# A three-layer graph network on one core: the rows of 57 gathered tiles are fetched one by one by SP and ScalarE

## The chip, the cores and the metric

The kernel runs on one core of one Trainium2 chip. The metric is the device time of one execution in microseconds (us), the median of several runs. The profile is one further execution, recorded by the hardware profiler.

Names of the profile: PE is TensorE (PEld its weight load), DVE is VectorE, ACT is ScalarE, POOL is GpSimd, SP is SyncE. A name with a q behind it (SPq, ACTq, DVEq) is that engine's instruction queue: DMA issues, register work, semaphore waits.

## The reference: what is computed

`x` has 6250 rows (nodes) of 256 floats; 100,000 edges, sorted by their target node, have a source, a target, one of 3 types and 32 attributes. All is float32.

```python
def _gcn_forward(x, edge_index, edge_type, edge_attr, weights, roots, biases, edge_w, edge_b):
    src, dst = edge_index
    ew = edge_attr @ edge_w + edge_b
    rel_masks = [(edge_type == i).astype(x.dtype) for i in range(3)]
    inv_cnt = [1.0 / jnp.maximum(segment_sum(m, dst, n), 1.0) for m in rel_masks]
    for l in range(3):
        residual = x
        msg = relu(x[src] * ew)
        out = zeros((n, 256))
        for i in range(3):
            h = segment_sum(msg * rel_masks[i][:, None], dst, n) * inv_cnt[i][:, None]
            out = out + h @ weights[l, i]
        x = residual + relu(out + x @ roots[l] + biases[l])
    return x
# the result is layernorm(x + _gcn_forward(x, ...))
```

The part that matters here is `x[src]`: in each of the three layers, 100,000 rows of 1 KB are fetched by index.

## The kernel before, in words

The edges are cut into 782 tiles of 128 edges (one edge per partition), two tiles to a pair, 391 pairs; two pairs lie together in one buffer `xs` of 128 x 2 x 2 x 256 floats (L895, eight such buffers). The function `layer` is called three times. Its main loop (L760) is written out in full and runs over steps `it`; each step reduces one pair, in the order `order`: pairs 64 to 390, then 63 down to 0. All instructions are recorded in this program order and each engine runs its own in that order; nothing reorders them later. So an engine that waits in one instruction holds back all that stands behind it on that engine.

What one step holds, with the pair that it serves counted from the step:

- `gather`, nine pairs ahead (L763, L898): GpSimd issues two indirect DMAs, each of which fetches 128 rows of `x` (first layer) or of `x_mid` (the layer before, written to DRAM) by the indices in `src_io`. The first six pairs of a layer are gathered at the end of the layer before.
- `load_at` on SP, when the pair nine ahead opens a new group of eight pairs (L559): the edge attributes, 256 KB. In the first layer ScalarE's queue loads blocks of `x` now and then (L545).
- `reduce`, this pair (L640): TensorE multiplies the messages `xs` with one-hot matrices `oh` of 120 columns (3 types x a window of 40 nodes) into PSUM `h_p`, two buffers.
- `make_ew`, four pairs ahead, once for four pairs (L594): TensorE makes the edge weights `ew_p` of four pairs in four PSUM banks from `at`.
- `add`, the pair before (L649): VectorE adds `h_p` to its window of `acc`, at a place held in a register; the registers are loaded eight at a time (L652).
- `weigh`, three pairs ahead, once for two pairs (L623): VectorE multiplies `xs` by `ew_p`, one instruction of 128 x 512 for each pair (L626); ScalarE takes the Relu of both pairs (L628).
- for one of 49 blocks of 128 nodes, about every eighth step: `root_turn` (TensorE transposes `x_all`, L664), one step later `root_turned` (ScalarE copies the result to `t_s`, L668), one step later `root_mul` (TensorE, L672), one step later `root_keep` (VectorE, L675).
- for a block whose edges are done: `node_mul` (TensorE, L687) and `node_end` (VectorE, L718 and L721), each in two parts; SP writes the block to `x_mid` (L723), or in the last layer to the output (L740) after the norm; ScalarE clears its place in `acc` (L704, L707). In the last layer SP also loads the block of `x` again (L747).
- `one_hot`, two pairs ahead, once for two pairs (L630): VectorE makes `oh`, in the first layer ScalarE a bfloat16 copy `oh_b` (L638).

Of the kernel before, what the change touches and what calls it, by code (L numbers as in the profile page):

```python
# [8 lines left out]
F32 = mybir.dt.float32  # L9
BF = mybir.dt.bfloat16  # L10
I32 = mybir.dt.int32
# [431 lines left out]
def ordered_path(ctx, tc, x, attr_laid, A, weights, roots, biases, edge_w, edge_b, out, src, src_i, seg, place_i, consts, x_root,  # L443
# [6 lines left out]
    nc = tc.nc  # L450
    P = 128
    N, D = x.shape
# [10 lines left out]
    order, _, moved, least, most = schedule(N, E, 1)  # L463
# [19 lines left out]
    with tc.tile_pool(name="bias_s", bufs=1) as bias_s:  # L483
# [9 lines left out]
        rows_of = bias_s.tile([P, D], F32, name="rows_of")  # L493
# [34 lines left out]
    edge = ctx.enter_context(tc.tile_pool(name="edge", bufs=2))  # L528
# [7 lines left out]
    def first_of(p, n):  # L536
        return p == 0 or order[p - 1] // n != order[p] // n
# [19 lines left out]
    def load_at(g):  # L557
        at = edge.tile([P, GROUP // OCT, 2, P], F32, name="at", bufs=3)
        nc.sync.dma_start(at.rearrange("p o i e -> p (o i e)"), attr_laid[g])  # L559
        return at  # L560

    def find_came():
        e = 2 * P * order[0]
        nc.scalar.dma_start(came_i.rearrange("p t e -> p (t e)"),
                            src[e:e + 2 * FIRST * P][None, :].to_broadcast([P, 2 * FIRST * P]))
        for t in range(2 * FIRST):
            nc.vector.tensor_scalar(came[:, t, :], came_i[:, t, :], node_i[:, 0:1], None, op0=ALU.is_equal)

    def layer(l, r_sb, b_sb, ats, early, pools):
# [5 lines left out]
        x_rows = x if l == 0 else x_mid[l - 1]  # L575
        w_sb = wpool.tile([P, R * DC, D], F32, name="w_sb")
        CH = DC + 1 if l == 0 else DC
        xs, ew_ps, ohs, h_ps, o_ps, rs = {}, {}, {}, {}, {}, {}
        x0s, mvs, oh_bs, t_ss, places = {}, {}, {}, {}, []
        r_next, ats_next, early_next = (None, None), {}, {}  # L580

        def gather(u):
            p = order.index(u)
            if p < FIRST:
                xs[u // 2] = early[u // 2]
            else:
                if first_of(p, 2):
                    xs[u // 2] = room(rows, D)
                gather_pair(nc, xs[u // 2], x_rows, src_i, u)

        def pairs_of(q):
            return range(min(2, U - 2 * q))
# [15 lines left out]
        def gather_early(p):  # L608
            u = order[p]
            if first_of(p, 2):  # L610
                early_next[u // 2] = room(rows, D)
            gather_pair(nc, early_next[u // 2], x_mid[l], src_i, u)

        def complete(q):
            for k in pairs_of(q):
# [4 lines left out]
                                     start=True, stop=True)  # L620
                nc.vector.tensor_add(xs[q][:, k], rest, xs[q][:, k])

        def weigh(q, pairs=None):  # L623
            pairs = pairs_of(q) if pairs is None else pairs
            for k in pairs:
                nc.vector.tensor_mul(xs[q][:, k], ew_ps[2 * q + k], xs[q][:, k])  # L626
            there = xs[q][:, pairs.start:pairs.stop]
            nc.scalar.activation(there, there, AF.Relu)  # L628

# [112 lines left out]
        def load_x0(c):  # L742
            n = min(P, N - c * P)
            x0s[c] = edge.tile([P, D], F32, name="x0", bufs=2)
            if n < P:
                nc.vector.memset(x0s[c], 0.0)
            nc.sync.dma_start(x0s[c][:n, :], x[c * P:c * P + n, :])  # L747
# [12 lines left out]
        for it in range(-11, max(starts) + 7):  # L760
            def pair(k):
                return order[it + k] if 0 <= it + k < U else None
            if pair(AHEAD) is not None:  # L763
                gather(pair(AHEAD))
            if l < L - 1 and 0 <= it + AHEAD - U < FIRST:
                gather_early(it + AHEAD - U)
            if l == 0 and it == 20:
                find_came()
            if pair(AHEAD) is not None and pair(AHEAD) // GROUP not in ats:
                ats[pair(AHEAD) // GROUP] = load_at(pair(AHEAD) // GROUP)  # L770
            if l == 0 and it >= -4 and (it + 4) % 20 == 0 and (it + 4) // 20 * 6 < NT - 1:
                load_x((it + 4) // 20 * 6)
            if it == 10:
                nc.sync.dma_start(w_sb, weights[l].rearrange("r (c p) e -> p (r c) e", p=P))
            if l == L - 1 and it + 2 in root_at:
                load_x0(root_at[it + 2])
            if l < L - 1 and it == U - 10:
                r_next = load_root(l + 1)
            if l < L - 1 and U - 10 <= it < U - 8:
                ats_next[at_groups[it - U + 10]] = load_at(at_groups[it - U + 10])  # L780

            if pair(0) is not None:
                reduce(pair(0))
            if pair(4) is not None and first_of(it + 4, OCT):
                make_ew(pair(4) // OCT)
            if pair(-LAG) is not None:
                add(pair(-LAG))
            if pair(3) is not None and first_of(it + 3, 2):
                if l > 0 and it + 3 < FIRST:
                    complete(pair(3) // 2)  # L790
                if pair(3) // 2 != order[-1] // 2:
                    weigh(pair(3) // 2)

            if pair(3) is not None and pair(3) // 2 == order[-1] // 2:
                weigh(pair(3) // 2, range(pair(3) % 2, pair(3) % 2 + 1))
            if it in root_at:
                root_turn(root_at[it])
            if it - 1 in root_at:
                root_turned(root_at[it - 1])
            if it - 2 in root_at:  # L800
                root_mul(root_at[it - 2])
            if it - 3 in root_at:
                root_keep(root_at[it - 3])
            if it == moved:
                move()
            if it - 2 == moved:
                clear(P)
            if it + 1 in node_at and slot_of(node_at[it + 1]) == 0:
                wrap()
            if it in node_at:  # L810
                node_mul(node_at[it], 0)
            if it - 1 in node_at:
                node_end(node_at[it - 1], 0)
            if it - 2 in node_at:
                node_mul(node_at[it - 2], 1)
            if it - 3 in node_at:
                node_end(node_at[it - 3], 1)
                clear(slot_of(node_at[it - 3]))
            if it - 4 in node_at and l == L - 1:
                deviate(node_at[it - 4])  # L820
            if it - 5 in node_at and l == L - 1:
                norm(node_at[it - 5])
            if pair(2) is not None and first_of(it + 2, 2):
                one_hot(pair(2) // 2)
# [68 lines left out]
def room(rows, D):  # L893

    return rows.tile([128, 2, 2, D], F32, name="xs", bufs=ROWS)  # L895


def gather_pair(nc, xs, x_rows, src_i, u):  # L898
    for i in range(2):
        nc.gpsimd.indirect_dma_start(  # L900
            out=xs[:, u % 2, i, :], out_offset=None, in_=x_rows[:, :],
            in_offset=bass.IndirectOffsetOnAxis(ap=src_i[:, 2 * u + i:2 * u + i + 1], axis=0))
# [162 lines left out]
```

## Time and profile before

| | |
|---|---|
| median of 3 runs | 3693.74 us (3690.77 to 3698.78) |
| profiled execution | 3692.14 us, span 3690.3 us |
| instructions in the profile | 54932 |
| busy DVE, ACT | 2082.3 us (56%), 935.3 us (25%) |
| busy POOL | 2244.9 us (61%), 2355 instructions |
| mean granted TensorE clock | 0.843 |
| DMA packets, bytes | 173323, 387.87 MB, mean 105 GB/s |
| DMA queues' share of 16 engines | GpSimd's 28.9%, SP's 5.7%, ScalarE's 0.7% |

The span runs from the first to the last instruction of the profile. A group line names the source line, the engine, the operation, what it writes and reads (`out<-in`, buffer numbers left out), and the count (x); then the busy time in us and the mean of one in ns, then the idle time of that engine just before such instructions, and what ended most of it. A waits line reads "who waited <- for whom: us in total, times, longest". A timeline line has the start and the length in us, and in brackets the idle time before it. In the chain in order of time each piece has a start, a length and what it is. Matmul ends are modelled by the profiler, not observed.

### The profile page before, as it was taken

Reading aid. Unit: us, or ns where it says so; the run is one execution under the profiler, and the core shown is the slowest. Engines: PE = TensorE matmul, PEld = TensorE weight load, DVE = VectorE, ACT = ScalarE, POOL = GpSimd, SP = SyncE. Lnnn points to the kernel's source line nnn. Section 1 sums busy time; section 2 is a strip of 40 time slices with the busy share of each in tenths; the row PEclk is TensorE's granted clock in tenths of the full one; section 3 lists DMA queues with packets and bytes.
Section 4 is the critical chain, followed back from the end, with each engine's and each line's share of the span. In section 5 each row is a group of like instructions: output and inputs, shape, how many; then the busy total and the mean of one; then the engine's idle time right before and its main releaser. Section 6 shows DMA issues by size and latency. Waiting matters only on the chain.

```text
span 3690.3 us, 54932 instructions
## 1 busy us (share of the span) xinstructions
PE 2687.3 (73%) x18875; PEld 2261.2 (61%) x18875; DVE 2082.3 (56%) x5868; ACT 935.3 (25%) x1155; POOL 2244.9 (61%) x2355
## 2 busy tenths in 40 slices
PE   3777877888886667777777777665777777777766
PEld 3666666666666556666666656555666666666655
DVE  4555655566665445555555555544555656666655
ACT  2233333333333222222222222211222222222221
POOL 5666665665566556666666666656666666666664
PEclk9788888888888778888889889787888888888887
DMA  4333333333333333333333333333333333333332
GB/s 129 117 109 119 106 111 98 102 106 103 100 107 106 98 90 100 98 104 104 104 100 106 107 107 104 104 96 112 109 113 113 106 109 111 105 105 107 107 105 67
DMA packets 173323, 387.87 MB, mean 105 GB/s; under 512 B 43418, under 2 KB 78636, under 8 KB 173036
## 3 DMA queue, kind: packets, MB, share of 16 engines
q0 software_dynamic: 112608, 307.65, 28.9%
q1 hardware_dynamic: 53136, 68.50, 5.7%
q10 hardware_dynamic: 7292, 8.11, 0.7%
q8 instruction: 154, 2.52, 0.3%
q14 instruction: 133, 1.09, 0.1%
HBM read 364.62 MB, written 19.46 MB: 104 GB/s over the span
## 4 chain that ended last, share of the span: by engine, by line
PE 49%; another core or an unknown queue 12%; DVE 11%; issue 8%; POOL 1%; DMA 1%; DVEq 1%; ACT 1%; POOLq 0%; ACTq 0%
PE h_p L644 27%; PE o_p L687 10%; PE ew_p L605 6%; DVE xs L626 4%; DVE acc L659 3%; PE r_p L672 3%; PE ew_p L601 2%; DVE x_root L718 2%; DVE oh L634 2%; POOL xs L900 1%; DMA xs<-x_mid,src_io 1%; PE r_p L664 1%; DVE x_all L721 0%; DVEq L659 0%
## 5 line engine op out<-in xcount | busy, mean ns | idle before, releaser
L644 PE MATMUL h_p<-oh,xs 128*128 128x120 f32 x9336 | 1544.9, 317 | 735.5 <-DVE acc L659 485.0
L900 POOL DMA_INDIRECT xs<-x_mid,src_io x1564 | 1497.1, 957 | 930.4 <-issue 810.2
L644 PEld LDWEIGHTS h_p<-oh,xs 128*128 128x128 f32 x9336 | 1400.5, 225 | 916.5 <-DVE acc L659 535.5
L626 DVE TENSOR_TENSOR xs<-ew_p,xs 128x512 f32<-128x512 f32 x1167 | 756.2, 682 | 871.4 <-PE h_p L644 340.3
L628 ACT ACTIVATE xs<-xs 128x1024 f32<-128x1024 f32 (+1 forms) x588 | 617.6, 1050 | 2396.8 <-DVE xs L626 2190.7
L900 POOL DMA_INDIRECT xs<-in_x_dram,src_io x770 | 734.1, 953 | 475.2 <-issue 413.0
L659 DVE TENSOR_TENSOR acc<-h_p,acc 128x240 f32 (+1 forms) x1173 | 518.1, 442 | 448.1 <-remote 255.6
L687 PE MATMUL o_p<-w_sb,acc 128*128 128x256 f32 (+1 forms) x1716 | 523.6, 446 | 109.5 <-DVE x_root L718 57.1
L634 DVE TENSOR_SCALAR oh<-iota_w,seg_o 128x120 f32<-128x120 f32 x2346 | 518.7, 295 | 0.0
L687 PEld LDWEIGHTS o_p<-w_sb,acc 128*128 128x128 f32 (+1 forms) x1716 | 359.0, 223 | 205.8 <-issue 62.9
L605 PE MATMUL ew_p<-ew_sb,at 32*128 32x256 f32 x4692 | 361.8, 426 | 4.4 <-issue 4.4
L605 PEld LDWEIGHTS ew_p<-ew_sb,at 32*128 32x128 f32 x4692 | 275.2, 220 | 42.3 <-issue 12.6
L718 DVE SCALAR_TENSOR_TENSOR x_root<-o_p,inv,x_root 128x256 f32<-128x256 f32 (+1 forms) x429 | 206.0, 480 | 121.6 <-PE o_p L687 42.6
L672 PE MATMUL r_p<-r_sb,t_s 128*128 128x256 f32 x588 | 185.2, 438 | 81.7 <-ACT t_s L668 68.4
L672 PEld LDWEIGHTS r_p<-r_sb,t_s 128*128 128x128 f32 x588 | 113.8, 216 | 104.5 <-ACT t_s L668 74.5
L638 ACT ACTIVATE oh_b<-oh 128x480 bf16<-128x480 f32 x196 | 117.8, 601 | 197.4 <-DVE oh L634 152.2
L704 ACT ACTIVATE acc<-zero_o 128x768 f32<-128x768 f32 (+1 forms) x150 | 140.8, 938 | 74.2 <-PE r_p L687 17.9
L601 PE MATMUL ew_p<-bias,full_ones 3*128 3x512 bf16 x1173 | 142.6, 453 | 21.4 <-issue 17.7
L644 PE MATMUL h_p<-oh_b,full_ones 128*128 128x120 bf16 x782 | 120.1, 238 | 10.0 <-issue 9.6
L644 PEld LDWEIGHTS <-full_ones 128*128 128x128 bf16 x782 | 89.8, 115 | 23.1 <-issue 17.1
L664 PE MATMUL r_p<-ident_o,x_all 128*128 128x128 f32 x294 | 73.2, 340 | 0.0
L675 DVE TENSOR_TENSOR x_root<-r_p,b_sb 128x256 f32<-128x256 f32 x147 | 61.1, 415 | 19.6 <-PE r_p L672 8.5
(92 smaller groups left out, 485.8 us busy)
## 6 DMA issues: line engine op xcount, KB each, us to landing
at<-in_attr_laid_dram SPq DMA_DIRECT2D x147, 256.0 KB
xs<-x_mid,src_io POOLq DMA_INDIRECT x1564
xs<-in_x_dram,src_io POOLq DMA_INDIRECT x770
x_mid<-x_all SPq DMA_DIRECT2D x96, 128.0 KB
x_all<-in_x_dram ACTq DMA_DIRECT2D x8, 768.0 KB
x<-in_x_dram SPq DMA_DIRECT2D x48, 128.0 KB
out_dram<-x_all SPq DMA_DIRECT2D x48, 128.0 KB
w_sb<-in_L_gnn_weights_dram SPq DMA_DIRECT2D x3, 768.0 KB
```

The lines of the kernel that those rows point to most:

```text
L601: nc.tensor.matmul(banks[j].rearrange("p i d -> p (i d)"), full_ones[j * A:j * A + PARTS, :], bias[j * A:j * A + PARTS].rearrange("p i d - ...
L605: nc.tensor.matmul(banks[j][:, i, :], ats[OCT * o // GROUP][j * A:(j + 1) * A, o % (GROUP // OCT), i, :], ew_sb[j * A:(j + 1) * A, :], sta ...
L626: nc.vector.tensor_mul(xs[q][:, k], ew_ps[2 * q + k], xs[q][:, k])
L628: nc.scalar.activation(there, there, AF.Relu)
L634: nc.vector.tensor_scalar(ohs[q][:, t, :], iota_w, seg[:, 4 * q + t:4 * q + t + 1], None, op0=ALU.is_equal)
L644: nc.tensor.matmul(h_ps[u][:, d, :], xs[u // 2][:, u % 2, i, d * P:(d + 1) * P] if d < DC else full_ones, (ohs if d < DC else oh_bs)[u // ...
L659: nc.vector.tensor_tensor(there, h_ps[u][:, :CH].rearrange("p c (r w) -> p c r w", r=R), there, op=ALU.add)
L672: nc.tensor.matmul(rs[c][:, 1, :], t_ss[c][:, d, :], r_sb[:, d, :], start=(d == 0), stop=(d == DC - 1))
L687: nc.tensor.matmul(o_p[:n, j, :], acc[:, d, r, slot:slot + n], w_sb[:, r * DC + d, :], start=(d == 0), stop=(d == DC - 1))
L704: nc.scalar.activation(acc[:, :CH, :, slot:slot + P], zero[:, :, None, None].to_broadcast([P, CH, R, P]), AF.Copy)
L718: nc.vector.scalar_tensor_tensor(root, o_p[:n, j, :], inv[:n, c, r:r + 1], root, op0=ALU.mult, op1=ALU.add)
L900: nc.gpsimd.indirect_dma_start(out=xs[:, u % 2, i, :], out_offset=None, in_=x_rows[:, :], in_offset=bass.IndirectOffsetOnAxis(ap=src_i[:, ...
```

## The change

Two instruction queues get a part of the gathering. A plan, made while the program is written out, gives single tiles of 128 rows to SP (first tile of the first pair of a buffer) and to ScalarE (second tile of the second pair). SP takes 4 rows per step, so 32 steps for a tile, from step 6 of a layer on, one tile after another: 11 tiles a layer, 33 in all, over 352 of the 391 steps. ScalarE takes 3 rows per step, 43 steps for a tile, from step 10 on: 8 tiles a layer, 24 in all, over 344 steps. A planned tile is used at the earliest six steps after its last rows were asked for, in the step's own count, that is by `weigh` three pairs ahead some four steps after.

For each such tile:

- four steps before, SP loads its 128 indices into one partition (`index`, 512 bytes);
- for every eight rows the lending engine loads eight registers from `index`; for every row it works out the address (one register instruction of two multiplications) and issues a DMA of one row (1 KB) from `x` or `x_mid` to one partition of a buffer `lent` (two per engine). These stand at the start of the step, right behind GpSimd's gathers, so on ScalarE ahead of the step's ACTIVATEs and on SP ahead of its other DMAs;
- GpSimd leaves that tile out;
- `weigh` splits the pair's multiplication in two of 128 x 256: one reads `lent`, the other `xs`. Both write to `xs`, so all behind them is as before.

In the built program GpSimd has 2289 gathers where it had 2346; SP has 4281 more DMAs (4224 rows, 57 index loads), 528 more register loads and 4224 more register computations; ScalarE 3072 more DMAs, 384 more register loads and 3072 more register computations; VectorE 57 more multiplications and 114 more semaphore instructions. TensorE's and ScalarE's other work is the same, in the same order.

```diff
+        hands = [(queue, kind, rate, buffers, lent_to(order, N, P, j, rate))
+                 for j, (queue, kind, rate, buffers) in enumerate(HANDS_OF(nc))]
+        lent = {(q, k, i): None for hand in hands for _, q, k, i in hand[-1]}
+        indices, values = {}, {}
+        def lend(it):
+            for j, (queue, kind, rate, buffers, plan) in enumerate(hands):
+                for s, q, k, i in plan:
+                    if it == s - 4:
+                        e = (4 * q + 2 * k + i) * P
+                        indices[q] = edge.tile([1, P], I32, name=f"index{j}", bufs=2)
+                        nc.sync.dma_start(indices[q], src[e:e + P][None, :])
+                    if not s <= it < s + -(-P // rate):
+                        continue
+                    if it == s:
+                        lent[q, k, i] = edge.tile([P, D], F32, name=f"lent{j}", bufs=buffers)
+                    for r in range((it - s) * rate, min(P, (it - s + 1) * rate)):
+                        if r % 8 == 0:
+                            _, values[j] = nc.values_load_multi_w_load_instructions(
+                                indices[q][0:1, r:r + 8], engines=[kind], min_val=0, max_val=N - 1,
+                                skip_runtime_bounds_check_because="each source is a node")
+                        queue.dma_start(lent[q, k, i][r:r + 1, :], x_rows[bass.ds(values[j][r % 8], 1), :])
...
+        def parts(q, k):
+            return [(0, 1), (1, 1)] if any((q, k, i) in lent for i in range(2)) else [(0, 2)]
         def weigh(q, pairs=None):
             pairs = pairs_of(q) if pairs is None else pairs
             for k in pairs:
-                nc.vector.tensor_mul(xs[q][:, k], ew_ps[2 * q + k], xs[q][:, k])
+                for i, n in parts(q, k):
+                    there = xs[q][:, k, i:i + n]
+                    rows_of = lent.get((q, k, i))
+                    nc.vector.tensor_mul(there, ew_ps[2 * q + k][:, i:i + n],
+                                         there if rows_of is None else rows_of[:, None, :])
...
             if pair(AHEAD) is not None:
                 gather(pair(AHEAD))
+            lend(it)
...
+def lent_to(order, N, P, j, rate):
+    steps = -(-P // rate)
+    plan, s = [], 6 + 4 * j
+    while True:
+        p = s + steps + 6
+        while p + 1 < len(order) and (order[p] // 2 != order[p + 1] // 2 or order[p] // 2 == order[p - 1] // 2):
+            p += 1
+        if p + 12 > len(order):
+            return plan
+        q = order[p] // 2
+        plan.append((s, q, j, j))
+        s += steps
+def HANDS_OF(nc):
+    return ((nc.sync, mybir.EngineType.SP, 4, 2), (nc.scalar, mybir.EngineType.Activation, 3, 2))
-def gather_pair(nc, xs, x_rows, src_i, u):
+def gather_pair(nc, xs, x_rows, src_i, u, lent=()):
     for i in range(2):
+        if (u // 2, u % 2, i) in lent:
+            continue
         nc.gpsimd.indirect_dma_start(
```

More of the change, by code (lines that the diff above doesn't have):

```diff
@@ L588, in gather @@
                     xs[u // 2] = room(rows, D)
-                gather_pair(nc, xs[u // 2], x_rows, src_i, u)
+                gather_pair(nc, xs[u // 2], x_rows, src_i, u, lent)
         def pairs_of(q):
```

## The prediction, made before the changed kernel was run

> **What bounds the kernel now.** I read the page's busy shares and chain first, then the chain in order of time around 1800 us, then the list of waits, then the two gather lines by stretches.
>
> ```profile
> span 3690.3 us, 54932 instructions
> PE 2687.3 (73%) x18875; PEld 2261.2 (61%) x18875; DVE 2082.3 (56%) x5868; ACT 935.3 (25%) x1155; POOL 2244.9 (61%) x2355
> ...
> PE 49%; another core or an unknown queue 12%; DVE 11%; issue 8%; POOL 1%; DMA 1%; DVEq 1%; ACT 1%; POOLq 0%; ACTq 0%
> ```
>
> The chain is half TensorE; 12% more has no named owner. One such piece, from the chain between 1800 and 1830 us, and ScalarE's row at its end, from the timeline:
>
> ```profile
> 1804.06 0.69 DVE xs L626
> 1804.75 3.57 another core or an unknown queue
> ...
> 1808.35 0.49 DVE x_root L718
> ```
>
> ```profile
> 1808.34 0.84 ACT L704 ACTIVATE acc<-zero_o 128x768 f32<-128x768 f32 x1 [2.50 <-remote]
> ```
>
> For 3.57 us the chain names nobody, and at its end VectorE's L718 and ScalarE's L704 start within 10 ns. Both wait for products of TensorE (L687), whose ends the page models only, so I read the piece as TensorE finishing later than drawn. TensorE then has about 49 + 12 of 100 parts of the chain, VectorE 11. TensorE sets the end, with VectorE behind it in the short stretches between.
>
> Is GpSimd, which the change relieves, on the path? Its groups, three rows of its timeline, and the waits:
>
> ```profile
> L644 PE MATMUL h_p<-oh,xs 128*128 128x120 f32 x9336 | 1544.9, 317 | 735.5 <-DVE acc L659 485.0
> L900 POOL DMA_INDIRECT xs<-x_mid,src_io x1564 | 1497.1, 957 | 930.4 <-issue 810.2
> ...
> L900 POOL DMA_INDIRECT xs<-in_x_dram,src_io x770 | 734.1, 953 | 475.2 <-issue 413.0
> ```
>
> ```profile
> 1804.49 0.94 POOL L900 DMA_INDIRECT xs<-x_mid,src_io  x1 [0.30 <-issue]
> 1805.74 0.95 POOL L900 DMA_INDIRECT xs<-x_mid,src_io  x1 [0.30 <-issue]
> ...
> 1809.14 0.95 POOL L900 DMA_INDIRECT xs<-x_mid,src_io  x1 [2.45 <-issue]
> ```
>
> ```profile
> POOL xs L900 <- issue: 1223.1, 2184, 6.9
> ...
> PE h_p L644 <- DVE acc L659: 485.0, 191, 5.5
> ...
> PEld r_p L672 <- ACT t_s L668: 74.5, 21, 6.6
> ...
> PE r_p L672 <- ACT t_s L668: 68.4, 19, 6.4
> ```
>
> Gathers in a row start 1.25 us apart (0.95 drawn, 0.30 between). All 2346 need 2346 x 1.25 = 2933 us of the span's 3690; so GpSimd has some 750 us over, and shows them as stops like the 2.45 us at 1809.14, which end just after TensorE's products came. It is ahead and waits for a free `xs` buffer. How far ahead, the counts by stretches show: the gathers of L900, then the multiplications of L626 that use them.
>
> ```profile
> 0.00:600.00 600.00, 364.23 (x382) 0.87 0.38 115
> 600.00:1250.00 650.00, 393.39 (x413) 0.84 0.35 103
> ```
>
> ```profile
> 0.00:600.00 600.00, 116.58 (x180) 0.87 0.38 115
> 600.00:1250.00 650.00, 133.48 (x207) 0.84 0.35 103
> ```
>
> By 600 us there are 382 gathers, 191 pairs of tiles, and 180 pairs are multiplied; by 1250 us 397.5 against 387. GpSimd runs 10 to 11 pairs ahead. There are 1173 pairs, one per step of 3690 / 1173 = 3.15 us: a lead of 33 us. The waits hold no row in which VectorE waits for a gather of `xs`.
>
> **What goes.** 57 of 2346 gathers, 57 x 1.25 = 71 us of GpSimd. With the lead above, what falls due next is the same `xs` buffer, freed by the same L644: I cost the gain at nothing. Were that cover gone, it would be 71 us.
>
> **What VectorE gets.** For 57 pairs the one multiplication over 128x512 becomes two over 128x256. The nearest row for the half is L675, the same operation from PSUM and SBUF at that size.
>
> ```profile
> L626 DVE TENSOR_TENSOR xs<-ew_p,xs 128x512 f32<-128x512 f32 x1167 | 756.2, 682 | 871.4 <-PE h_p L644 340.3
> ...
> L675 DVE TENSOR_TENSOR x_root<-r_p,b_sb 128x256 f32<-128x256 f32 x147 | 61.1, 415 | 19.6 <-PE r_p L672 8.5
> ```
>
> ```profile
> L659 DVEq FUSED_REGOPS  x1170: 69/69/69, 53.3 to 3676.2; - x195
> L659 DVEq EVENT_SEMAPHORE  x952: 21/21/1471, 67.3 to 3677.8; - x191
> ```
>
> (2 x 0.415 - 0.682) x 57 = 8.4 us, and the build has 114 more semaphore instructions there at 0.021 us, 2.4 us: 10.8 us. VectorE is on the path only between TensorE's long pieces, so from 0 to all of it counts; I take half, 5 us.
>
> **What a lent row costs its queue.** Each is a register computation and a DMA, and each eight rows a load of eight registers. No one-row DMA is in this trace. The nearest are ScalarE's four small loads of 32 rows back to back, SP's writes and loads of 128 rows, and the register rows:
>
> ```profile
> 16.15 1.75 ACTq L481 DMA_DIRECT2D ew_sb<-in_L_gnn_edge_w_dram  x4
> 17.94 0.43 ACTq L485 DMA_DIRECT2D left<-in_L_gnn_edge_b_dram  x1
> ```
>
> ```profile
> L723 SPq DMA_DIRECT2D x_mid<-x_all x98: 246/320/331, 187.7 to 2474.3; - x98
> ```
>
> ```profile
> L559 SPq DMA_DIRECT2D at<-in_attr_laid_dram x147: 4/383/1715, 25.6 to 3617.1; - x147
> ```
>
> ```profile
> L652 DVEq TENSOR_LOAD <-place_i x147: 593/597/1049, 52.6 to 3668.5; - x147
> ```
>
> ```profile
> L1010 SPq TENSOR_LOAD <-flag x1: 463/463/463, 12.9 to 12.9; - x1
> ...
> L1010 SPq FUSED_REGOPS  x1: 186/186/186, 13.5 to 13.5; - x1
> ```
>
> (17.94 - 16.15) / 4 = 0.448 us from one DMA to the next; with 0.069 for the registers (L659) and 0.597 / 8 = 0.075 for the load, 0.59 us per row. Lower end: 0.246 (the shortest, 106 rows) + 0.069 + 0.075 = 0.39; upper: 0.448 + 0.186 + 0.075 = 0.71. I take 0.59, as the small load on ScalarE's own queue is the nearest form.
> [...]
>
> SP: 4 rows a step x 0.59 = 2.4 us, plus its own DMAs, 147 (L559), 98 (L723) and 2 x 49 blocks read and written in the last layer, 343 in 1173 steps x 0.4 = 0.12: 2.5 of 3.15 us, in 352 of 391 steps of a layer. It fits. What is moved behind rows on SP: the `at` loads (due 5 steps, 16 us, later at L605), the writes of `x_mid` (read in the next layer) and of the output (lending stops 33 steps before the end of each layer). The rows in turn stand behind those writes, for which SP waits in line:
>
> ```profile
> SPq L723 <- DVE x_all L721: 1231.2, 62, 53.2
> ```
>
> A write of L723 waits for the end of its step on VectorE, so SP starts the next step's rows a step late at worst. The first multiplication that needs a tile is 4 steps, 12.6 us, after its last rows: covered, if a row lands in time. The nearest landing: ScalarE's DMA of 17.94 lets VectorE start at
>
> ```profile
> 21.37 0.29 DVE L497 CAST part<-left 128x256 bf16<-128x256 f32 x1 [0.26 <-DMA left<-in_L_gnn_edge_b_dram]
> ```
>
> 3.4 us for 128 rows; a single row lies between nothing and that. The build also gives all DMAs of both queues eight completion counters in turn, and each waits until the one eight before it has landed: at 7 rows a step that one was issued 8 / 7 x 3.15 = 3.6 us earlier. On the mean it has landed; a queue that falls behind can hold up the other.
>
> ScalarE: 3 x 0.59 = 1.8 us a step, in 344 of 391 steps. Its own work stands in the same queue, behind the rows: the Relu (L628), `oh_b` (L638, first layer), the copy `t_s` (L668) and the clearing.
>
> ```profile
> L628 ACT ACTIVATE xs<-xs 128x1024 f32<-128x1024 f32 (+1 forms) x588 | 617.6, 1050 | 2396.8 <-DVE xs L626 2190.7 <-issue 196.4 <-DMA xs<-x_mid,src_io 7.2
> ...
> L668 ACT ACTIVATE t_s<-r_p 128x256 f32<-128x256 f32 x147 | 53.9, 367 | 4.9 <-remote 4.3 <-PE h_p L644 0.6
> ```
>
> ```profile
> 100.76 1.06 ACT L628 ACTIVATE xs<-xs 128x1024 f32<-128x1024 f32 x1 [0.98 <-DVE xs L626]
> 100.77 0.39 ACTq L545 DMA_DIRECT2D x_all<-in_x_dram  x1
> ```
>
> The last two rows show that a DMA starts as the ACTIVATE before it starts, and runs beneath it. Two steps hold one Relu: 3.6 us of rows against 4.1 us of idle before it (2396.8 / 588) and 1.05 us of its own run. The Relu thus mostly stays hidden, and TensorE needs it three steps later. `t_s` is the weak point: TensorE transposes in one step, ScalarE copies in the next, TensorE multiplies (L672) in the one after, so only one step is to spare; and TensorE already waits for it 19 to 21 times, 68 to 75 us in all. Each of those 21 waits lengthens by up to one step's rows: 21 x 1.8 x 344 / 391 = 33 us. The other 126 copies I take as covered.
>
> **Sum.** 0 + 5 + 33 = +38 us. The profiled execution took 3692.1 us (span 3690.3), the median of the runs is 3693.7: 3692.1 + 38 = 3730 against that execution, 3732 against the median. With a row at 0.39 us and hidden beneath the ACTIVATEs the sum falls to VectorE's 0 to 11; at 0.71 us to 5 + 40, and with VectorE whole 51. Waits of the other 126 copies, one in three by 1 us, would add 40 more.
>
> **Rivals.**
> *A queue becomes the bound.* SP's step is full when a row costs (3.15 - 0.12) / 4 = 0.76 us. Above 0.71 a row could come if the two queues hold each other up: seven DMAs one after another are 7 x 0.448 = 3.1 us, a full step before the register work, 4 x 0.144 = 0.6 us on SP, which would make 3.7. At 3.2 to 3.7 us a step the 3 x 352 steps of lending grow by 0.05 to 0.55 us, 50 to 580 us; the middle gives 3694 + 315 = 4010. For it: the lengths at the top of L559 (1.7 us). Against: no two DMAs of SP and ScalarE lie together in this trace but the first. [...]
> *Hidden.* The rows stay beneath the ACTIVATEs and in ScalarE's idle time, and TensorE's own pace covers VectorE's half. Decides where a row costs under 0.39 us, 1.2 us a step, near the Relu's 1.05. Not slower: 3694, between 3687 and 3701.
> *The gathers did pace it.* Then 71 us come off: 3694 - 71 + 5 = 3628. Place: GpSimd's 1.25 us per gather. It decides where GpSimd has no lead; 33 us of lead speak against it. This one is faster.
> *It doesn't do what it says:* the build has 2289 gathers and 7296 one-row DMAs, so it does; no chance.
>
> **How the numbers follow.** Forecast, slower by 8 to 130 us: 0.59, time 3732, and its own range 3702 to 3825. Queue bound: 0.21, half of it above 3900. Hidden: 0.14. Gathers: 0.06. Range 3690 to 3900: leaves out the gathers' 0.06, some 0.10 of the queue's and a few hundredths of the hidden case. About 0.2% (7 us) is what a measurement of this kernel can tell from no change. Faster by more 0.06, within 0.14, slower 0.80.
>
> **What would show it.** GpSimd: fewer gathers, equal 1.25 us apart, the rest as longer stops; lead still over 20 us. VectorE: 114 halves at about 0.415 us. SP and ScalarE: one-row DMAs about 0.45 us apart plus registers; above 0.76 a row, the queue rival is right. TensorE: the waits of L672 for `t_s` grow from 70 towards 105 us, those of L644 for L628 stay few. I am wrong if VectorE waits for `lent`, if L644 waits for the Relu by hundreds of us, or if the span shrinks.

## The result and the profile after

The changed kernel took 4133.94 us (median of 4 runs, 4124.10 to 4148.77) against 3694.15 of the kernel before: a ratio of 1.1193, 95% interval 1.1155 to 1.1231, 440 us slower. The forecast was +38 us, and the range ended at 3900.

One thing has to be said before anything is compared. The experiments ran in six groups, each group on one chip with the kernel before beside it. In three groups that kernel took 3693 to 3745 us, as in the result; in the other three it took 2985 or 2986. I call them the 3.7 ms groups and the 3.0 ms groups, and compare within a group unless I say otherwise. The result belongs to the first kind. What makes the kind is not known. The record numbers the groups' chips 15, 7, 6, 0, 6 and 11, and number 6 stands beside 2986 us in the third group and 3695 us in the fifth: either the kind is no property of a chip, or two chips have that number.

Head of the page and TensorE's largest group, changed kernel (lines above 610 have moved: L626 is now L656, L628 L659, L644 L675, L605 L629, L672 L703, L723 L754):

```profile
span 4136.8 us, 77991 instructions
PE 2817.8 (68%) x18875; PEld 2332.1 (56%) x18875; DVE 2089.6 (51%) x5925; ACT 946.5 (23%) x1155; POOL 2185.1 (53%) x2298
...
L675 PE MATMUL h_p<-oh,xs 128*128 128x120 f32 x9336 | 1555.5, 320 | 589.7 <-issue 346.2
```

Every engine but SP, which the page doesn't count, is less busy as a share than before. GpSimd has more room, not less: it is idle before its gathers for 1292.4 + 617.8 us, where it was 930.4 + 475.2, so the 71 us taken off it bought nothing. The wait lists tell where the time went (total, times, longest):

```profile
PE ew_p L629 <- DMA at<-in_attr_laid_dram: 257.5, 53, 10.7
...
PE r_p L703 <- ACT t_s L699: 126.4, 39, 12.1
...
ACT xs L659 <- DMA lent<-x_mid: 685.8, 160, 11.4
...
DVE xs L656 <- DMA lent<-x_mid: 68.0, 15, 12.2
```

```profile
SPq L754 <- DVE x_all L752: 54.2, 8, 18.6
```

TensorE waits 257.5 us for `at`, which it never did. ScalarE stands 685.8 us in front of a Relu, held in its line by the rows ahead of it. The last row is the telling one. Before, SP stood at the write of `x_mid` for 1231.2 us waiting for VectorE: it was early. Now it waits 54.2: it is hardly ever early, it is the late one. Its rows say why. First one line's instructions, then two adjoining windows of SP's timeline, all of the changed kernel (`x7` is seven DMAs, 2.91 us from the first's start to the last's end):

```profile
L604 SPq FUSED_REGOPS  x4224: 2/37/1432, 31.7 to 4056.7; - x192
L604 SPq MOVE lent<-x_mid x2816: 1/29/1405, 1391.6 to 4056.7; - x188
L604 SPq DMA_DIRECT2D lent<-x_mid x2816: 2/228/1392, 1391.7 to 4056.8; - x188
```

```profile
2007.41 2.91 SPq L604 DMA_DIRECT2D lent<-x_mid  x7
```

```profile
2009.91 9.29 SPq L604 DMA_DIRECT2D lent<-x_mid  x9
```

A row is three instructions, a register computation, a register move and the DMA (37, 29 and 228 ns in the middle, min/median/max), and every eighth has a load of eight registers besides. In the first window rows begin 0.41 us apart. In the second, one stretch later, 9 rows take 9.3 us. The records of that stretch (start in us, ns, instruction):

```
2010.34    14 FUSED_REGOPS
2011.04    16 MOVE
2011.07     5 DMA_DIRECT2D
2011.76    16 TENSOR_LOAD
2011.79    37 FUSED_REGOPS
2011.86   655 MOVE
2012.53    13 DMA_DIRECT2D
2012.54    13 FUSED_REGOPS
2012.56   697 MOVE
2013.26    13 DMA_DIRECT2D
2013.28    13 FUSED_REGOPS
2013.30   674 MOVE
```

One to three instructions pass, of whatever kind, and then 0.7 us go by. For none of the 4224 register moves does the trace list a semaphore or a transfer to wait for. 1615 register instructions have over 0.4 us to the next start, together 1325 us of the span. Of these, 750 (613 us) stand before a move; the others stand before a DMA, and a DMA can wait: SP's wait list has 57.0 + 23.0 us of L604 for DMAs of `lent`. In e11 below, the same kernel in a 3.0 ms group, the numbers are 218 and 208 us, all of them before a DMA. On average the rows begin 0.91 us apart, so four take 3.64 us; 33 tiles x 128 rows x 0.91 us are some 3840 of the 4137 us. SP is full.

The lengths in such a stretch can hardly be what the instructions took. A row's DMA has 5 and 13 ns there and a load of eight registers 16, where e11 has no row's DMA under 224 ns and no such load under 689. In the changed kernel's trace 1113 of SP's 4224 row DMAs are under 100 ns.

The granted clock fell from 0.843 to 0.801, while TensorE is idle 4136.8 - 2817.8 = 1319 us in place of 1003. Its weight loads around a stop, in the kernel before:

```profile
1364.70 1.08 PEld L644 LDWEIGHTS h_p<-oh,xs 128*128 128x128 f32 x8
1370.21 1.78 PEld L644 LDWEIGHTS h_p<-oh,xs 128*128 128x128 f32 x8 [4.44 <-DVE acc L659]
```

The same eight loads take 1.08 us before a stop of 4.4 us and 1.78 after it. The granted clock in the trace is 1.00 from 1361.5 us and 0.50 from 1368.4 us, some 2.5 us into the stop, until 1375.2 us. Why it falls there was not shown.

### The profile page after: what moved, and what is told of

The parts are those of the page before. It is cut to its first block, busy times and chain, and to the rows that moved or that the text cites. A ratio compares the mean times of both kernels' runs of the same rounds, so it can differ in the third digit from the quotient of the medians.

```text
span 4136.8 us, 77991 instructions
## 1 busy us (share of the span) xinstructions
PE 2817.8 (68%) x18875; PEld 2332.1 (56%) x18875; DVE 2089.6 (51%) x5925; ACT 946.5 (23%) x1155; POOL 2185.1 (53%) x2298
## 5 line engine op out<-in xcount | busy, mean ns | idle before, releaser
L953 POOL DMA_INDIRECT xs<-x_mid,src_io x1526 | 1455.3, 954 | 1292.4 <-issue 956.3
L675 PE MATMUL h_p<-oh,xs 128*128 128x120 f32 x9336 | 1555.5, 320 | 589.7 <-issue 346.2
L675 PEld LDWEIGHTS h_p<-oh,xs 128*128 128x128 f32 x9336 | 1425.7, 229 | 780.0 <-issue 472.0
L659 ACT ACTIVATE xs<-xs 128x1024 f32<-128x1024 f32 (+1 forms) x588 | 618.1, 1051 | 2468.1 <-DVE xs L656 1130.4
L953 POOL DMA_INDIRECT xs<-in_x_dram,src_io x751 | 715.4, 953 | 617.8 <-issue 429.7
L656 DVE TENSOR_TENSOR xs<-ew_p,xs 128x512 f32<-128x512 f32 (+1 forms) x1167 | 736.1, 670 | 545.0 <-PE ew_p L629 190.5
L629 PE MATMUL ew_p<-ew_sb,at 32*128 32x256 f32 x4692 | 415.5, 459 | 293.0 <-DMA at<-in_attr_laid_dram 257.5
L718 PE MATMUL o_p<-w_sb,acc 128*128 128x256 f32 (+1 forms) x1716 | 535.6, 455 | 105.5 <-DVE x_root L749 41.3
L629 PEld LDWEIGHTS ew_p<-ew_sb,at 32*128 32x128 f32 x4692 | 285.6, 227 | 360.8 <-DMA at<-in_attr_laid_dram 281.1
L718 PEld LDWEIGHTS o_p<-w_sb,acc 128*128 128x128 f32 (+1 forms) x1716 | 370.7, 230 | 201.8 <-issue 65.7
L703 PE MATMUL r_p<-r_sb,t_s 128*128 128x256 f32 x588 | 229.3, 524 | 210.3 <-ACT t_s L699 126.4
L703 PEld LDWEIGHTS r_p<-r_sb,t_s 128*128 128x128 f32 x588 | 136.0, 256 | 251.7 <-ACT t_s L699 136.4
L675 PE MATMUL h_p<-oh_b,full_ones 128*128 128x120 bf16 x782 | 117.3, 236 | 53.7 <-issue 34.0
L675 PEld LDWEIGHTS <-full_ones 128*128 128x128 bf16 x782 | 89.2, 114 | 71.1 <-issue 65.6
L699 ACT ACTIVATE t_s<-r_p 128x256 f32<-128x256 f32 x147 | 55.8, 379 | 227.2 <-DMA lent<-x_mid 92.7
```

Source lines behind the costliest of these rows:

```text
L629: nc.tensor.matmul(banks[j][:, i, :], ats[OCT * o // GROUP][j * A:(j + 1) * A, o % (GROUP // OCT), i, :], ew_sb[j * A:(j + 1) * A, :], sta ...
L656: nc.vector.tensor_mul(there, ew_ps[2 * q + k][:, i:i + n], there if rows_of is None else rows_of[:, None, :])
L675: nc.tensor.matmul(h_ps[u][:, d, :], xs[u // 2][:, u % 2, i, d * P:(d + 1) * P] if d < DC else full_ones, (ohs if d < DC else oh_bs)[u // ...
L703: nc.tensor.matmul(rs[c][:, 1, :], t_ss[c][:, d, :], r_sb[:, d, :], start=(d == 0), stop=(d == DC - 1))
L718: nc.tensor.matmul(o_p[:n, j, :], acc[:, d, r, slot:slot + n], w_sb[:, r * DC + d, :], start=(d == 0), stop=(d == DC - 1))
L953: nc.gpsimd.indirect_dma_start(out=xs[:, u % 2, i, :], out_offset=None, in_=x_rows[:, :], in_offset=bass.IndirectOffsetOnAxis(ap=src_i[:, ...
```

## The experiments

The theories, by the letters of the expectations: **A** and **E**, SP's line is full by itself, E adding that the price is paid per instruction; **B**, the two queues hold each other up (the mechanism of the prediction's queue rival); **C**, ScalarE's own line paces; **D**, in the result's executions the engines get their instructions late, in others not; **F**, the DMA, not the instruction, is dear; **G** and **H**, the loss reaches TensorE through `at`, or through the rows themselves.

All ratios are to the kernel before in the same group, with their 95% intervals. "Row" is the mean distance of SP's rows within a tile, from their starts in the trace.

| run | on it | us | before | ratio | SP row, us |
|---|---|---|---|---|---|
| e1, e9 | SP alone | 2948, 2947 | 2985, 2986 | 0.987 [0.986, 0.989] both | 0.61 |
| e2, e10 | ScalarE alone | 2956, 2956 | 2985, 2986 | 0.990 [0.989, 0.992], 0.990 [0.988, 0.992] | - |
| e3 | split only | 2989 | 2985 | 1.001 [1.000, 1.002] | - |
| e4, e8 | constant rows | 2916, 2916 | 2985, 2986 | 0.977 [0.976, 0.979], 0.976 [0.975, 0.978] | 0.61 |
| e11 | the change | 2949 | 2986 | 0.987 [0.986, 0.989] | 0.63 |
| e18 | no gathers | 2738 | 2985 | 0.917 [0.916, 0.919] | 0.60 |
| e5 | the change | 4142 | 3693 | 1.123 [1.120, 1.125] | 0.91 |
| e6 | before | 3696 | 3693 | - | - |
| e7 | 2 and 2 rows a step | 3802 | 3693 | 1.029 [1.027, 1.031] | 1.65 |
| e16 | 3 and 3 rows a step | 3883 | 3695 | 1.052 [1.048, 1.057] | 1.13 |
| e17 | split only | 3695 | 3695 | 1.000 [0.999, 1.001] | - |
| e12 | constant rows | 3807 | 3745 | 1.017 [1.015, 1.020] | 0.82 |
| e13 | SP alone | 4038 | 3745 | 1.076 [1.073, 1.080] | 0.89 |
| e14 | ScalarE alone | 3816 | 3745 | 1.020 [1.016, 1.023] | - |
| e15 | `at` by GpSimd | 4040 | 3745 | 1.078 [1.076, 1.081] | 0.89 |

**The first group, of the 3.0 ms kind.** The edits, each to the changed kernel:

```diff
 e1:-    return ((nc.sync, mybir.EngineType.SP, 4, 2), (nc.scalar, mybir.EngineType.Activation, 3, 2))
 e1:+    return ((nc.sync, mybir.EngineType.SP, 4, 2),)
 e2:+    return ((nc.scalar, mybir.EngineType.Activation, 3, 2),)
 e3:     lend() issues nothing; gather(u) has, for a tile in lent:
 e3:+        there = lent[u // 2, u % 2, i] = edge.tile([P, D], F32, name=f"lent{i}", bufs=2)
 e3:+        nc.gpsimd.indirect_dma_start(out=there, ...)
 e4:-    queue.dma_start(lent[q, k, i][r:r + 1, :], x_rows[bass.ds(values[j][r % 8], 1), :])
 e4:+    queue.dma_start(lent[q, k, i][r:r + 1, :], x_rows[r:r + 1, :])      (and no register loads)
```

> Only SP fetches rows (33 tiles, 4 rows per step); ScalarE fetches none and GpSimd gathers its 24 tiles. Theory A, SP's line is full by itself: in the changed kernel SP's rows begin 0.91 us apart on average, so 4 rows take 3.6 us of a 3.15 us step, and 1056 such steps lose some 440 us. Then the time stays near 4100 us (4040 to 4140) and the rows stay 0.85 to 0.91 us apart. Rival B, the two queues hold each other up through the eight completion counters that they take in turn: without ScalarE's rows SP's are under 0.76 us apart and the time is 3700 to 3770 us. In between: both have a share.

> Only ScalarE fetches rows (24 tiles or so, 3 rows per step); SP keeps its old work and the loads of the lists. Theory A: ScalarE's rows cost only what they put ahead of the copies of line 699, 33 us by the prediction, and the held-back Relu is hidden: 3715 to 3760 us. Rival B (coupling through the counters): near 3700 to 3740, the same, as no other queue has many transfers. Rival C, ScalarE's own line is what paces, its Relu coming too late for TensorE: 3900 us or more, TensorE waiting for line 659 or VectorE for line 656's buffers.

> No rows one by one: GpSimd gathers all tiles as before, but the 57 tiles go to the lent buffers, so that VectorE multiplies their pairs in two halves. It measures the prediction's 10.8 us of VectorE work alone. All theories but one: 3694 to 3710 us. If the split halves set back VectorE's order of work by more than their own time: over 3730 us.

> The same one-row DMAs on SP and ScalarE, of the same size, but with row r of the table as a constant source (other rows than the reference's are fetched): no register loads, no register instructions; one instruction for a row instead of three and an eighth. Theory A1, the row is dear because of its register instructions: rows are 0.25 to 0.45 us apart, SP fits in its step, and the time is 3700 to 3760 us. Rival A2, the DMA itself is dear (its completion counters, its descriptors): rows are still over 0.75 us apart in a full stretch and the time is 3900 us or more.

Both halves of the change made the kernel faster here, which none of the expectations had. Constant rows gain 2985 - 2916 = 69 us, and 57 gathers x 1.25 us are 71: in this group the gathers do pace. The page of the split kernel, whose work is that of before, shows it in the chain:

```profile
POOL 28%; PE 26%; DMA 19%; issue 18%; DVE 7%; ACT 2%; DVEq 0%; POOLq 0%; ACTq 0%
```

and VectorE waits for them (the split kernel in a 3.7 ms group, e17, has 2.9 us of this, once):

```profile
DVE xs L648 <- DMA xs<-x_mid,src_io: 452.9, 325, 4.5
DVE xs L648 <- DMA xs<-in_x_dram,src_io: 193.8, 139, 5.1
```

**The second group, of the 3.7 ms kind.** e5 is the changed kernel, e6 the one before, and e7 differs by `SP, 2, 2` and `Activation, 2, 2`.

> The changed kernel itself again. In the runs with SP alone, ScalarE alone and constant rows, the kernel before took 2985 us beside them, where it took 3694 us beside the changed kernel, and their records show none of the waits of some 0.7 us between SP's register instructions that the changed kernel's profile is full of, and fewer in TensorE's. Theory D, in the result's executions the engines got their instructions late, and the 22,000 instructions that the change adds made that worse: where instructions come on time, SP's rows are 0.5 us apart, SP fits, and the change gives the gathers' time back, some 70 us: a ratio of 0.975 to 0.985 to the kernel before, if that is again near 2985 us; if it is near 3694 us, again 1.12. Theory A, the two queues together are too much anywhere: a ratio of 1.05 or more in either case.

> The kernel before itself, for a profile of it beside these runs. Theory D: near 2985 us, TensorE's idle time put down to issue and to remote is under half of the 228.6 and 24.2 us of line 644 in the profile of before, no run of matmuls with starts 0.7 us apart, and the gathers' chain (line 900) is a large part of the chain that ended last, where it was 1%. If it is near 3694 us again: the same profile as before.

> Both queues fetch 2 rows per step, so about half the tiles on SP and two thirds on ScalarE. If instructions come late in these executions (before near 3694 us): SP, with 2 rows of 0.9 us in 3.15 us, is no longer the bound, and the loss falls from 440 us to under 130 us. If they come on time (before near 2985 us): GpSimd is relieved of some 31 tiles of 1.25 us, a gain of some 35 us, ratio 0.985 to 0.993.

The result came again, and so did the profile of before. At half the rate the loss is 109 us, under the 130 expected.

**The third group, again of the 3.0 ms kind.** e8, e9 and e10 are e4, e1 and e2 once more.

> The same one-row DMAs with row r of the table as a constant source (so other rows than the reference's are fetched), once more. Where the kernel before takes near 3694 us: theory E, SP is slowed per instruction (in stretches that fill a third of the time, two or three instructions pass in 0.7 us, whatever they are). With 1 instruction a row in place of 3.1, a row takes 0.27 us in two thirds of the time and under 0.7 us in the other third, mean under 0.5 us; SP fits in its step and the time is 3650 to 3760 us. Rival F, what is slow is the DMA (its completion, its descriptor): rows stay over 0.8 us apart, 4000 us or more. Where the kernel before takes near 2985 us: 2916 us again.

> Rows on SP alone, once more. Where the kernel before takes near 3694 us: theory E says SP's line is full by itself, 0.9 us a row, 4050 to 4130 us. Rival B, the queues hold each other up through the shared counters: without ScalarE's rows under 3850 us. Where the kernel before takes near 2985 us: 2948 us again.

> Rows on ScalarE alone, once more. Where the kernel before takes near 3694 us: by theory E the SP queue is free, `at` loads come in time, and only the copies of line 699 are held up: 3715 to 3780 us. Rival C, ScalarE's line is slowed as SP's and its Relu comes late: 3900 us or more. Where the kernel before takes near 2985 us: 2956 us again.

> The changed kernel beside these three, on the same chip. Where the kernel before takes near 3694 us: 1.12 again. Where it takes near 2985 us: by theory D/E the rows are 0.5 to 0.6 us apart, SP keeps up, and the time is that of the constant rows or a little more, 2915 to 2950 us, a gain of 1.2 to 2.3%; if the two queues together are too much even there: over 3040 us.

The whole change is 1.3% faster in this group; 2949 us is near the upper end of the 2915 to 2950 that D and E said. The same line of the same program as above, here:

```profile
L604 SPq FUSED_REGOPS  x4224: 37/37/48, 33.6 to 2877.4; - x192
L604 SPq MOVE lent<-x_mid x2816: 29/29/29, 988.5 to 2877.5; - x188
L604 SPq DMA_DIRECT2D lent<-x_mid x2816: 224/228/419, 989.7 to 2877.5; - x188
```

All 2816 moves take 29 ns; in the result's trace one takes 1405. The distance of two rows is 0.41 us in the median where the result's trace has 0.65, and 0.63 in the mean instead of 0.91. The change gains 36 us, not the constant rows' 69: with 4 x 0.63 = 2.5 us SP fills the shorter step of 2949 / 1173 = 2.51 us too, and the page has "SPq 13%" in the chain. SP alone (e1, e9) gains as much as both.

**The fourth group, of the 3.7 ms kind, which decides.** e12, e13 and e14 are e4, e1 and e2; e15 has, in `load_at`:

```diff
-        nc.sync.dma_start(at.rearrange("p o i e -> p (o i e)"), attr_laid[g])
+        nc.gpsimd.dma_start(at.rearrange("p o i e -> p (o i e)"), attr_laid[g])
```

> The one-row DMAs with row r of the table as a constant source (other rows than the reference's are fetched). Where the kernel before takes near 3694 us: theory E, SP is slowed per instruction: with 1 instruction a row in place of 3.1 a row takes under 0.5 us on average, SP fits in its step, and the time is 3650 to 3760 us. Rival F, the DMA is what is slow: rows stay over 0.8 us apart, 4000 us or more. Where the kernel before takes near 2985 us: 2916 us again.

> Rows on SP alone. Where the kernel before takes near 3694 us: theory E says SP's line is full by itself, 0.9 us a row, 4050 to 4130 us. Rival B, the queues hold each other up through the shared counters: without ScalarE's rows under 3850 us. Where the kernel before takes near 2985 us: 2948 us again.

> Rows on ScalarE alone. Where the kernel before takes near 3694 us: by theory E the SP queue is free, `at` loads come in time, and only the copies of line 699 are held up: 3715 to 3780 us. Rival C, ScalarE's line is slowed as SP's and its Relu comes late: 3900 us or more. Where the kernel before takes near 2985 us: 2956 us again.

> The whole change, but the loads of `at` are issued by GpSimd, not by SP behind its rows. Where the kernel before takes near 3694 us: theory G, SP's lateness reaches TensorE chiefly through `at`: TensorE's 281 us of waiting for it vanish, the x_mid rows and the lent rows are still late, and the time falls to 3800 to 3950 us. Rival H, the late rows themselves pace (VectorE waits for the lent tile, the lines of SP being full in any case): over 4050 us, the wait moved to line 656 of VectorE. Where the kernel before takes near 2985 us: GpSimd paces there, and 147 more issues on it cost some 1 us each of which a part shows: 2950 to 3100 us.

Constant rows leave all 7296 one-row DMAs in and take out two of three instructions. The loss falls to 62 us (E said 3650 to 3760 beside 3694, at most 66 more; 3807 beside 3745 is within that). SP is early again; its waits, constant rows first, then SP alone with register rows:

```profile
SPq L750 <- DVE x_all L748: 402.8, 55, 49.1
```

```profile
SPq L754 <- DVE x_all L752: 25.5, 2, 12.9
```

And the slow steps are still there, but now on the only instruction left, the DMA itself, which in a 3.0 ms group (second fence, e4) never takes over 0.48 us:

```profile
L600 SPq DMA_DIRECT2D lent<-x_mid x2816: 2/250/1479, 1318.3 to 3711.2; - x188
```

```profile
L600 SPq DMA_DIRECT2D lent<-x_mid x2816: 214/250/478, 983.9 to 2819.2; - x188
```

So F falls and E holds: in these groups SP is slowed per instruction, and the change multiplied its instructions from 665 to 14,023. (F's spacing came, 0.82 us in the mean where E said under 0.5, but this is the step's own pace, as SP waits; the median is 0.33.) B falls too: without ScalarE's rows SP's are 0.89 us apart in place of 0.91. SP alone loses 293 us, less than the 356 to 436 that E's 4050 to 4130 meant beside 3694. ScalarE alone loses 71, within the 21 to 86 expected, so C falls. Together they would be 364 of the some 450 that the second group's ratio, 1.123, makes of 3745 us, so some 90 us come only with both. e15 halves the question: against that ratio of another group it has 1.078, so about a third of the loss went by way of `at`; the 295 us left lie between G (106 to 256) and H (over 356), and neither was right. TensorE waits for `at` once, 2.6 us, and VectorE waits longer for lent rows than in the change (68.0 there):

```profile
DVE xs L656 <- DMA lent<-x_mid: 112.1, 14, 14.5
```

**The fifth group, of the 3.7 ms kind.** e16 has `SP, 3, 2`; e17 is e3.

> SP fetches 3 rows in a step in place of 4 (24 tiles or so in place of 33), ScalarE 3 as before. Where the kernel before takes 3690 to 3750 us: by the theory of a full line, 3 rows of 0.9 us are 2.7 us of a 3.15 us step, so SP keeps up on average and the loss falls from 440 to 100 to 180 us (2 rows lost 109). If the loss goes with the number of rows and not with a threshold, it is 109 + (440 - 109) / 2, some 275 us. Where the kernel before takes near 2985 us: rows of 0.41 us and the loads make 3 x 0.51 = 1.5 of 2.5 us, GpSimd is relieved of some 48 gathers, 2930 to 2950 us.

> All tiles gathered by GpSimd, the 57 into the lent buffers, multiplied in halves. Where the kernel before takes 3690 to 3750 us: the prediction put 10.8 us on VectorE and 5 us on the end: a ratio of 1.000 to 1.004. If VectorE's order of work is set back by more than its own time: over 1.01. Where the kernel before takes near 2985 us: 1.001 again.

e16 lost 188 us, above the 100 to 180 expected of a threshold and well below a straight line's 275. SP's waits at `x_mid` with 2, 3 and 4 rows a step:

```profile
SPq L754 <- DVE x_all L752: 655.3, 71, 51.3
```

```profile
SPq L754 <- DVE x_all L752: 250.5, 49, 29.6
```

With 4 it is the 54.2 above: the room that SP has left shrinks, and is gone at 4. The loss is 109 us for 30 tiles on both queues, 188 for 48 and 440 for the change's 57, that is 3.6, 3.9 and 7.7 us per tile: even up to 3 rows, and twice as dear once SP is full. So a full line is not the whole loss: at 3 rows SP still waits 250.5 us for VectorE here and TensorE has no wait for `at`, yet 188 us are lost. One place of this rest is TensorE itself. Its idle time "on issue" before the `h_p` matmuls (L644, here L675) is 256.7 us in the kernel before and 458.5 in e7 of the same group, 242.4 in e17 and 382.7 in e16 beside it. All versions with one-row DMAs in the 3.7 ms groups have 382.7 to 486.6, ScalarE alone (e14) among them:

```profile
PE h_p L675 <- issue: 467.4, 480, 26.6
```

In the 3.0 ms groups it is 47.1 us at most. So instructions added on SP or ScalarE go with more slow steps on TensorE, whose own instructions are the same. How much of the loss that is can't be read off, as TensorE waits less for VectorE meanwhile (`acc`: 293.1 us in e14 against 485.0 before). e17 puts VectorE's split multiplications at 0.3 us, with 3.3 us less to 4.1 more inside the interval.

**The last run, in a 3.0 ms group.** It was to tell what SP's slow steps go with: `gather_pair` has a `memset` in place of the gather.

> The changed kernel with GpSimd filling the rows of the other tiles with zeros in place of gathering them (the gathers of those tiles are left out; the 57 tiles' rows are fetched as in the change). Where the kernel before takes 3690 to 3750 us: if the gathers' transfers are what slows SP's instructions, the moves of line 604 take 29 ns in nearly all cases, rows are 0.41 us apart in the median, and the time falls under 3300 us. If not, the median stays near 0.65 us, some moves still take up to 1400 ns, and SP's 4 rows of 0.9 us hold the time over 3900 us. Where the kernel before takes near 2985 us: SP's rows are undisturbed anyway, 0.6 us a row, and the time is bounded by TensorE's 2416 us and SP's 2.5 us a step, 2750 to 2950 us.

It met a group without slow steps, so it says nothing of them. It ended at 2738 us, 12 below what was expected there, with TensorE's 33% and SP's 20% in the chain; against the change's 2949 of the third group the other gathers are worth 7% there.

## Why the prediction was wrong, by its steps

**TensorE sets the end and GpSimd is ahead: right for the result.** GpSimd's stops grew by some 500 us and VectorE has no wait for a gather there, so costing the gain at nothing was right. In the 3.0 ms groups the rival in which the gathers pace is right, with its price (71 us against 69), and the whole change is faster. One profile can't carry that verdict to executions of the other kind.

**The unnamed 12% of the chain** I read as TensorE ending later than drawn. No run tests that reading, and I did not ask why it would be late. TensorE's own timeline in the kernel before had the pattern that later filled SP's:

```profile
1019.25 0.26 PE L644 MATMUL h_p<-oh,xs 128*128 128x120 f32 x1 [0.33 <-issue]
1019.96 0.36 PE L644 MATMUL h_p<-oh,xs 128*128 128x120 f32 x1 [0.45 <-issue]
1020.68 0.26 PE L644 MATMUL h_p<-oh,xs 128*128 128x120 f32 x1 [0.36 <-DMA xs<-in_x_dram,src_io]
1021.39 0.58 PE L644 MATMUL h_p<-oh,xs 128*128 128x120 f32 x3 [0.45 <-issue]
```

Matmuls that follow 0.11 us apart elsewhere begin 0.71, 0.72 and 0.71 us apart, mostly with nothing to wait for. "issue" against TensorE's L644 was 228.6 us. The split kernel, whose work is that of before, has this row in both kinds of group (3.0 ms first):

```profile
PE h_p L667 <- issue: 41.3, 51, 2.4
```

```profile
PE h_p L667 <- issue: 242.4, 300, 20.6
```

Idle time "on issue" was a sign that instructions are dear in these executions, and the change adds 23,000 of them.

**VectorE, +5 us: nothing** (e17). The halves came at the price taken:

```profile
L656 DVE TENSOR_TENSOR xs<-ew_p,lent 128x256 f32<-128x256 f32 x57 | 23.9, 419 | 96.3 <-DMA lent<-x_mid 68.0 <-PE h_p L675 12.2 <-remote 8.5
```

**The row, 0.59 us (0.39 to 0.71), "It fits": the step that failed.** Undisturbed, the price was good: 0.41 us and an eighth of a load of eight registers (0.78 us in the middle on SP, in a 3.0 ms group) make 0.51. The load was taken at VectorE's 0.60. But each end came from instructions that stood alone, with room behind them; none bounded what a long run of instructions costs when some of them are slow. In the result's trace a row was 0.91 us, over the 0.76 at which the text itself said SP is full, so the queue did not fit its step.

**`at`, due 16 us later, and the lent tiles, "covered": failed with it.** A lead covers a delay, not a rate. A queue that needs 3.64 us a step eats 16 us of lead within some 30 steps, then every `at` is late. The four steps of the lent tiles went the same way, and VectorE did wait for `lent`.

**ScalarE, +33 us through `t_s`: half the size, and not the place.** ScalarE alone loses 71 us, but TensorE's waits for `t_s` in e14 are 39.9 us, against 68.4 before. In the changed kernel, with SP's rows beside, they grew to 126.4, when ScalarE itself stands 685.8 + 281.2 us for rows where alone it stands 217.8 + 66.5. TensorE's wait of L675 for the Relu grew from 2.3 to 19.7 us only, few as expected. What makes the 71 us of ScalarE alone was not separated; TensorE's doubled idle time on issue, above, is the candidate that the trace offers.

**The queue rival, 50 to 580 us: right in place and price, wrong in mechanism.** It gave 4010 at its middle and the result is 4134. But it would come by the two queues holding each other up; SP alone has rows of 0.89 us against 0.91 (0.61 against 0.63 in the other groups), so sharing is worth 0.02 us a row, some 80 us over SP's 4224 rows at most. The price came out right by luck.

**What stays open:** why instructions of an engine wait 0.7 us in one group and not in another. In the changed kernel's trace the gathers' packets of 4096 bytes are in flight in some 60% of the slow time of SP in the first layer and in 37% of the rest of it, which is no proof, and the run that would have tried it met the other kind of group. Nor is it shown that the engine itself is slow: the too short lengths in the slow stretches would also fit a delay in recording the instructions that holds the engine up. The executions that the record lists one by one all have the profiler's span and granted clock, so they don't tell how long the kernels take without it. No version tried beats the kernel before in both kinds; in a 3.7 ms group none that fetches rows does.

## What to carry to other kernels

Price added work on an idle queue per instruction, and compare rate with rate: rows x price against the step; buffers ahead pay for a delay once and for a rate never. Before adding thousands of instructions, look whether the profile of before charges busy engines with idle time on "issue", and at what spacing. And a bottleneck argued from one profile holds for executions like it: here the same edit is 12% slower in one kind of group and 1.3% faster in the other.

## What the runs showed of the hardware

- In some groups of runs the records of an engine's instructions come one to three at a time with 0.7 us between, even register moves: 29 ns in the middle, up to 1405 (changed kernel); in others 29 ns in all 2816 cases (e11). TensorE shows the same spacing (0.71 us from 1019.25 us on in the kernel before), and its idle time on issue before the `h_p` matmuls is 458.5 us where SP and ScalarE fetch rows (e7), 256.7 in the kernel before beside it (e6).
- The kernel before itself takes 2985 us in the one kind of group and 3693 to 3745 in the other; its split form, within 0.2% of it, has a granted clock of 0.92 (e3) or 0.84 (e17), and GpSimd or TensorE as its bound.
- In the 3.0 ms groups a one-row DMA of 1 KB from a register address costs its queue 228 ns, or 0.41 us to the next with its two register instructions (e11); with a constant address 250 ns, 0.32 us to the next in the median (e4).
- A load of eight registers takes 0.78 us on SP and 0.83 on ScalarE (e11), against 0.60 on VectorE (kernel before, L652).
